# Graph layer 1 of a four-layer kernel: the row terms by sums on VectorE, a tile's own block of comparisons made by groups ahead, and part of the mask sums taken with the mask

## The chip, the cores and the metric

One core of one Trainium2 chip runs the whole program. The metric is the device time of one execution in microseconds (us), the median of the runs shown. The engines are named as the profile names them: PE (TensorE matmul), PEld (its weight load), DVE (VectorE), ACT (ScalarE), POOL (GpSimd), SP (SyncE, which here only issues transfers). Each engine works through its own queue in order.

## The reference, cut to what matters

Four graph layers run one after the other on `x` (2708 x 128) with a matrix `adj` (2708 x 2708); every layer begins with `h = relu(layernorm(x))` and adds its output to `x`. Layer 0 has a sum over each node's four nearest neighbours beside `adj @ h`. The change is in layer 1:

```
XW = h @ W
s_col = XW @ a[0, :128];  s_row = XW @ a[0, 128:]
den = exp(leaky_relu(s_row[:, None] + s_col[None, :], 0.01))
num = adj @ den
att = where(num != 0, den / num, 0)
x = x + adj @ (att @ XW)
```

`s_row` and `s_col` hold one number for each node. In the kernel they are called the row term (`r_nat`, node on the partition; `row_all`, the same numbers along the free axis, repeated on all partitions) and the column term (`c_nat`).

## The kernel before, in words

The 2708 nodes are 22 tiles of 128 (the last has 20), and six groups of four tiles (the last has two, 148 nodes). `adj` comes transposed, so a row tile of 128 x 2708 numbers, 1354 KB, is one "chunk".

**Second aggregation of layer 0** (`aggregate(y2, done_l0, kept=4)`, L597). For 17 chunks PE multiplies as they arrive, then for five chunks that stay in SBUF it goes bank by bank (L255). After bank b it calls `done_l0(b-1)`: copy to SBUF on ACT (L564), turn back by four PE transposes (L222), add to `xs` on DVE (L558), layer norm (L171 to L181), late neighbour terms (L524, gathered by POOL, L518), and `terms` of the group before.

**Row terms** (`terms`, L570). A group of `h1` is transposed on PE and copied to `hT` (L211, L214); a product with `rep`, the vector W a[128:] repeated 128 times (L429), gives the row term on every partition (L577), which ACT copies to `row_all` (L578); four PE transposes of one row bring it back to nodes on partitions (L580), in one PSUM bank that DVE copies to `r_nat` when all six groups are there (L599, L600).

**Places** (`place`, L656, for t = 0 to 21). The kernel sorts the nodes by row term by counting. DVE makes a 0/1 mask of the comparisons of tile t with itself and with all later tiles: the own block in two instructions with ties by node number (L662, L665), the rest in one (L669). ACT sums the mask along the row (L670, `later`). PE sums it down the columns into PSUM, bank by bank (L677). After each group of four tiles `places_of` copies one row of the counts (L690), turns it (L694), adds (L701, L706) and POOL scatters the nodes to their places in DRAM (L711, 22 scatters). The sorted list comes back at L822 and is turned at L824.

**Totals** (`total`, L736). Between the places PE forms `w_n @ adj` chunk by chunk (L744), with `w_n` from ACT (L635), which needs `r_nat` and its maximum. Nine chunks are still in SBUF (four in the pool `big`, five in row buffers); 13 are loaded again (L733): one at once into a free layer buffer, four into `big`, eight into the five row buffers, each load after the total that frees its buffer. Ten totals go with t = 1 to 10, one with each even t after that, the rest behind the places.

**Column terms** (`column_terms`, L754): 22 PE products of one column (L757), copied by DVE to `c_nat` (L758, L759). They are written after place 4, but the planner, which orders each engine's instructions by what is ready, puts them among the last row terms.

**Knots.** After the last total, DVE and ACT finish `tots` (L857, L858), four small transfers put it into `first` (its other parts are set by memsets, L859 to L861), and 22 gathers of sorted rows (L843) feed PE (L933) to the end of that loop; its first product needs the sorted list, `tots` and `first`.

`pin` keeps an instruction at its place in program order; the others are ordered by the planner.

Of the kernel before, what the change touches and what calls it, by code (L numbers as in the profile page):

```python
# [9 lines left out]
F32 = mybir.dt.float32  # L10
# [15 lines left out]
def kernel(  # L26
# [136 lines left out]
    def layernorm_relu(dst, g):  # L163

        t0, t1 = GROUPS[g]
        n = t1 - t0
        st = small.tile([P, 4, 6], F32, name="ln_st")
        mv = small.tile([P, 4, 2], F32, name="ln_mv")
        rs = small.tile([P, 4], F32, name="ln_rs")
        for t in range(t0, t1):  # L170
            nc.vector.bn_stats(st[:, t - t0, :], xs[:, t, :])  # L171
            nc.vector.bn_aggr(mv[:, t - t0, :], st[:, t - t0, :])
        root = nc.scalar.activation(rs[:, :n], mv[:, :n, 1], AF.Sqrt, bias=ln_eps)
        nc.vector.reciprocal(rs[:, :n], rs[:, :n])
        nm = small.tile([P, 4], F32, name="ln_nm")
        nc.vector.scalar_tensor_tensor(
            nm[:, :n], mv[:, :n, 0], -1.0, rs[:, :n], op0=ALU.mult, op1=ALU.mult
        )
        for t in range(t0, t1):
            o = t - t0  # L180
            nc.scalar.activation(  # L181
                dst[:, t, :],
                xs[:, t, :],
                AF.Relu,
                scale=rs[:, o : o + 1],
                bias=nm[:, o : o + 1],
            )
        return root
# [145 lines left out]
    for i in range(T):  # L334
# [4 lines left out]
        for b, (k0, n) in enumerate(KBS):  # L339
# [5 lines left out]
                start=(i == 0),  # L345
                stop=(i == T - 1),
            )
    sum_rows = res.tile([P, 1024], F32, name="sum_rows")
    for half, p0, p1 in ((0, 0, 128), (1, 0, 32 * (NKB - 5)), (1, 32 * (NKB - 5), 32 * (NKB - 4))):
        n = KBS[4 * half + p0 // 32][1]  # L350
        evacuate(sum_rows[p0:p1, 512 * half : 512 * half + n], sums[half][p0:p1, :n])
# [67 lines left out]

    wgT = consts.tile([P, P], F32, name="wgT")  # L420
    wga = consts.tile([P, 2], F32, name="wga")
    rep = consts.tile([P, P], F32, name="rep")
    p = ps_s.tile([P, 512], F32, name="ps")
    pin(nc.tensor.transpose(p[:, :P], wg, ident))
    nc.vector.tensor_copy(wgT, p[:, :P])
    p = ps_s.tile([P, 512], F32, name="ps")
    nc.tensor.matmul(p[:, :2], wgT, a_nat, start=True, stop=True)
    nc.vector.tensor_copy(wga, p[:, :2])
    nc.vector.tensor_scalar(rep, ones, wga[:, 1:2], None, op0=ALU.mult)  # L429

    top_v = keep.tile([P, T, 8], F32, name="top_v")
    top_i = keep.tile([P, T, 8], U32, name="top_i")
    strips = []
    nc.vector.memset(top_v[:, T - 1, :], 0.0)
    for t in range(T):
# [17 lines left out]
            nc.vector.max_index(top_i[:w, t, :], top_v[:w, t, :], s[:w, :])  # L455


    near_u = keep.tile([P, T, TOPK], U32, name="near_u")
    near_t = small.tile([P, T, TOPK], U32, name="near_t")

    def row_numbers(w, t0, t1):
# [7 lines left out]
        pin(nc.vector.max_index(top_i[:w, t, :], top_v[:w, t, :], strips[t][:w, :]))  # L469


    sim = keep.tile([P, T, TOPK], F32, name="sim")
    pin(
        nc.vector.scalar_tensor_tensor(
            sim, top_v[:, :, :TOPK], -2.0, sq.to_broadcast([P, T, TOPK]), op0=ALU.mult, op1=ALU.add
# [30 lines left out]
    row_numbers(TAIL, T - 1, T)  # L506


    simd = keep.tile([P, T, TOPK], F32, name="simd")
    nc.vector.tensor_tensor(  # L510
        simd, sim, dinv2[:, :, None].to_broadcast([P, T, TOPK]), ALU.mult
    )
# [1 line left out]
    def add_near(t, late=False):  # L514
        w = width(t)
        for k in range(TOPK):
            g = res.tile([P, D], F32, name="gath", bufs=32)
            nc.gpsimd.indirect_dma_start(  # L518
                out=g[:w, :],
                out_offset=None,  # L520
                in_=ydr[:, :],
                in_offset=bass.IndirectOffsetOnAxis(ap=near_u[:w, t, k : k + 1], axis=0),
            )
            term = nc.vector.scalar_tensor_tensor(  # L524
                xs[:w, t, :],
                g[:w, :],
                simd[:w, t, k : k + 1],
                xs[:w, t, :],
                op0=ALU.mult,
                op1=ALU.add,  # L530
            )
            if late and k == 0:
                pin(term)
# [25 lines left out]
            xs[:w, t, :], p, dinv2[:w, t : t + 1], xs[:w, t, :], op0=ALU.mult, op1=ALU.add  # L559
        )  # L560

    def to_h1(g, s2):
        k0, n = KBS[g]
        nc.scalar.copy(u2T[:, k0 : k0 + n], s2[g][:, :n])  # L564
        node_product(u2T, None, g, add_l0)
        return layernorm_relu(h1, g)

    r_ps = []

    def terms(g):  # L570
        t0, t1 = GROUPS[g]
        k0, n = KBS[g]
        if not r_ps:
            r_ps.append(acc(0))
        transposed(hT, h1, g, nc.scalar.copy)
        p = ps_s.tile([P, 512], F32, name="ps")
        nc.tensor.matmul(p[:, :n], rep, hT[:, k0 : k0 + n], start=True, stop=True)  # L577
        last = nc.scalar.copy(row_all[:, k0 : k0 + n], p[:, :n])  # L578
        for t in range(t0, t1):
            nc.tensor.transpose(  # L580
                r_ps[0][: width(t), t : t + 1], row_all[:1, cols(t)], ident[:1, :1]
            )
        return last


    late = {0: (15,), 1: (16,), 2: (17,), 3: (18, 19), 4: (20, 21)}

    def done_l0(g, s2):
        to_h1(g, s2)
        for t in late.get(g, ()):  # L590
            add_near(t, late=True)
        if g:
            terms(g - 1)

    for t in range(15):
        add_near(t)
    aggregate(y2, done_l0, kept=4)  # L597
    last_row = terms(NG - 1)
    pin(nc.vector.tensor_copy(r_nat[:, : T - 1], r_ps[0][:, : T - 1]))  # L599
    nc.vector.tensor_copy(r_nat[:TAIL, T - 1 :], r_ps[0][:TAIL, T - 1 : T])  # L600

    with tc.issue_after(last_row.ins):
        tables = nc.scalar.preload_act_table_set("natural_log_exp_and_others")
# [23 lines left out]
        nc.vector.tensor_reduce(top, p, AX.X, ALU.max)  # L627
        return top

    rmax = node_max("rmax", r_nat, r_ps[0][:, 256:384])  # L630
    r_n = vec("r_n")
    nc.vector.tensor_scalar(r_n, r_nat, rmax, None, op0=ALU.subtract)
    w_n = vec("w_n")
# [22 lines left out]
    def place(t):  # L656
        w = width(t)
        rt = r_nat[:w, t : t + 1]
        a, e = t * P, t * P + w
        mk = flags.tile([P, N], BF16, name="mask")  # L660
        eq = small.tile([P, P], F32, name="eq")
        nc.vector.scalar_tensor_tensor(  # L662
            eq[:w, :w], row_all[:w, a:e], rt, tri[:w, :w], op0=ALU.is_equal, op1=ALU.mult
        )
        nc.vector.scalar_tensor_tensor(  # L665
            mk[:w, a:e], row_all[:w, a:e], rt, eq[:w, :w], op0=ALU.is_le, op1=ALU.subtract
        )
        if e < N:
            nc.vector.tensor_scalar(mk[:w, e:], row_all[:w, e:], rt, None, op0=ALU.is_le)  # L669
            nc.scalar.activation(  # L670
                seen[:w, e:], mk[:w, e:], AF.Copy, accum_out=later[:w, t : t + 1]
            )
        for b, (k0, n) in enumerate(KBS):
            c0, c1 = max(a, k0), k0 + n
            if c0 < c1:
                g = 32 * (b % 4)
                nc.tensor.matmul(  # L677
                    cnt[b // 4][g : g + 32, c0 - k0 : c1 - k0],
                    ones_b[:w, :32],
                    mk[:w, c0:c1],  # L680
                    start=(t == 0),
                    stop=(e == c1),
                )

    def places_of(b):
        t0, t1 = GROUPS[b]
# [36 lines left out]
    def total_chunk(t, n):  # L723
        if t in resident:
            return resident.pop(t)
        if n == 0:
            c = lay.tile([P, N], F32, name="chunkY", tag="Y")
        elif n <= 4:
            c = big.tile([P, N + 1], F32, name="chunk", tag="big")
        else:  # L730
            c = rowtile("chunk")
        w = width(t)
        pin(nc.sync.dma_start(c[:w, :N], adjT[t * P : t * P + w, :]))  # L733
        return c
# [14 lines left out]
                    stop=(x_ == T - 1),  # L749
                )  # L750

    early = {todo[len(here)]: total_chunk(todo[len(here)], 0)}

    def column_terms():  # L754
        for t in range(T):
            w = width(t)
            nc.tensor.matmul(c_ps[:w, t : t + 1], hT[:, cols(t)], wga[:, 0:1], start=True, stop=True)  # L757
        nc.vector.tensor_copy(c_nat[:, : T - 1], c_ps[:, : T - 1])  # L758
        nc.vector.tensor_copy(c_nat[:TAIL, T - 1 :], c_ps[:TAIL, T - 1 : T])  # L759
        cmax = node_max("cmax", c_nat, c_ps[:, 384:512])  # L760
        nc.vector.tensor_scalar(cmx, cmax, rmax, -1.0, op0=ALU.add, op1=ALU.mult)
        c_n = vec("c_n")
        nc.vector.tensor_scalar(c_n, c_nat, rmax, None, op0=ALU.add)
        nc.vector.tensor_scalar(hb, c_n, 0.0, -0.495, op0=ALU.max, op1=ALU.mult)
        nc.scalar.activation(s_n, c_n, AF.Exp, scale=0.99)
        nc.scalar.activation(sig, hb, AF.Exp)
# [4 lines left out]
    for t in range(T):  # L771
        place(t)
        if t % 4 == 3 or t == T - 1:
            places_of(t // 4)
        if t == 4:
            column_terms()
        if 1 <= t <= len(here) + 1 or t % 2 == 0 and t:
            total(done)
            done += 1
    for x_ in range(done, T):  # L780
        total(x_)
    assert not resident
# [44 lines left out]
    nc.vector.tensor_copy(src_u[:PER, :], p[:PER, :T])  # L827
    nc.vector.tensor_copy(rs, p[:, T : 2 * T])

    moving = []

    def row_place():
        m = big.tile([P, N + 1], F32, name="mov", tag="big")
        moving.append(m)
        return m

    def fetch(t):
        m = moving[t] if t < len(moving) else row_place()  # L840
        if t:
# [8 lines left out]
        )  # L850


    first = row_place()
    tots = spare.tile([P, QUARTER], F32, name="tots", tag="spare")
    for half in range(2):
        x0 = tots[:, SPLIT * half : (SPLIT, QUARTER)[half]]
        nc.scalar.copy(x0, tot[half][:, : x0.shape[1]])  # L857
        nc.vector.scalar_tensor_tensor(x0, x0, 0.0, x0, op0=ALU.is_equal, op1=ALU.add)  # L858
    nc.vector.memset(first[0:1, :N], 0.0)  # L859
    nc.vector.memset(first[:, N : N + 1], 0.0)  # L860
    nc.vector.memset(first[0:1, N : N + 1], 1.0)  # L861
    for g in range(4):
        (nc.scalar, nc.sync)[g % 2].dma_start(
            first[1:2, QUARTER * g : QUARTER * (g + 1)], tots[32 * g : 32 * g + 1, :]
# [326 lines left out]
```

## Time and profile before

| | us |
|---|---|
| median of 3 runs | 1315.3 |
| lowest, highest | 1312.87, 1323.94 |
| profiled execution | 1309.14 |
| its span, first to last instruction | 1307.1 |
| PE busy in the span | 1085.9 |
| DVE busy | 560.4 |
| ACT busy | 411.7 |
| POOL busy | 228.1 |

All places in time below are us from the start of that span. The second aggregation runs from 349 to 543, the row terms from 526 to 561, the places and totals from 561 to 620, the knots from 630 to 787. A line of the table of windows gives for a stretch the busy time and the count of instructions of each engine, the clock that PE was granted (1.00 is full speed), the share of the DMA engines and their rate. A line of the timeline gives the start, the length, the engine, the line, the operation, the tiles, how many were merged, and in brackets how long the engine had been idle before and what ended that.

### The profile page before, as it was taken

Reading aid. Unit: us, or ns where it says so; the run is one execution under the profiler, and the core shown is the slowest. Engines: PE = TensorE matmul, PEld = TensorE weight load, DVE = VectorE, ACT = ScalarE, POOL = GpSimd, SP = SyncE. Lnnn points to the kernel's source line nnn. Section 1 sums busy time; section 2 is a strip of 40 time slices with the busy share of each in tenths; the row PEclk is TensorE's granted clock in tenths of the full one; section 3 lists DMA queues with packets and bytes.
Section 4 is the critical chain, followed back from the end, with each engine's and each line's share of the span. In section 5 each row is a group of like instructions: output and inputs, shape, how many; then the busy total and the mean of one; then the engine's idle time right before and its main releaser. Section 6 shows DMA issues by size and latency. Waiting matters only on the chain.

```text
span 1307.1 us, 10178 instructions
## 1 busy us (share of the span) xinstructions
PE 1085.9 (83%) x3623; PEld 510.2 (39%) x3623; DVE 560.4 (43%) x1178; ACT 411.7 (31%) x647; POOL 228.1 (17%) x188
## 2 busy tenths in 40 slices
PE   4889999999683359997777780687789999999998
PEld 1334444444240124553433330233344445545444
DVE  2020026999822000674465664899960031113003
ACT  3100014444400000585666743678830021003000
POOL 0100000000077720024211103567400000000000
PEclk8989999999795559887898985889989999999999
DMA  8997700000472242157999988999939916742831
GB/s 321 425 384 271 282 0 1 1 1 1 180 301 95 95 159 107 43 231 283 266 381 373 385 344 340 425 426 419 342 150 420 351 64 240 266 175 85 302 123 42
DMA packets 39505, 297.30 MB, mean 227 GB/s; under 512 B 6749, under 2 KB 10680, under 8 KB 13116
## 3 DMA queue, kind: packets, MB, share of 16 engines
q1 hardware_dynamic: 23806, 201.04, 40.2%
q0 software_dynamic: 13216, 93.62, 18.9%
q10 hardware_dynamic: 2434, 2.01, 0.6%
q8 instruction: 28, 0.46, 0.1%
q14 instruction: 21, 0.17, 0.0%
HBM read 264.46 MB, written 32.87 MB: 227 GB/s over the span
## 4 chain that ended last, share of the span: by engine, by line
PE 58%; DMA 18%; DVE 11%; issue 6%; another core or an unknown queue 6%; ACT 0%; POOL 0%; SPq 0%; ACTq 0%; DVEq 0%; POOLq 0%
PE acc L255 37%; DMA mov<-in_adj_dram,src_u 8%; PE acc L442 8%; DVE hi L1028 4%; DVE hi L1016 4%; DMA chunk<-in_adj_dram 3%; DMA hi<-table,hi_u 2%; PE acc L448 2%; PE acc L933 2%; PE ps L744 2%; DMA res<-in_adj_dram 2%; PE ps L224 1%; PE acc L1038 1%; PE ps L222 1%
## 5 line engine op out<-in xcount | busy, mean ns | idle before, releaser
L255 PE MATMUL acc<-chunk,y 128*128 128x512 f32 (+1 forms) x408 | 180.5, 592 | 73.2 <-issue 60.4
L1038 PE MATMUL acc<-hi,xw 128*128 128x512 f32 (+2 forms) x264 | 115.6, 594 | 65.6 <-DVE hi L1028 65.6
L255 PE MATMUL acc<-chunk,h 128*128 128x512 f32 (+1 forms) x384 | 148.0, 542 | 0.0
L255 PEld LDWEIGHTS acc<-chunk,y 128*128 128x128 f32 x408 | 79.6, 205 | 174.1 <-issue 162.4
L933 PE MATMUL acc<-mov,wt 128*128 128x512 f32 (+1 forms) x264 | 117.5, 600 | 34.7 <-DMA mov<-in_adj_dram,src_u 34.7
L518 POOL DMA_INDIRECT gath<-ydr,near_u x88 | 83.5, 949 | 346.5 <-DMA ydr<-y 320.0
L442 PE MATMUL acc<-zT 128*128 128x512 f32 (+2 forms) x264 | 107.6, 552 | 0.0
L1038 PEld LDWEIGHTS acc<-hi,xw 128*128 128x128 f32 (+1 forms) x264 | 52.1, 205 | 129.0 <-DVE hi L1028 69.3
L937 DVE COPY mov<-acc 2x512 f32<-2x512 f32 (+1 forms) x126 | 74.4, 611 | 63.8 <-PE acc L933 62.1
L255 PEld LDWEIGHTS acc<-chunk,h 128*128 128x128 f32 x384 | 68.8, 190 | 74.1 <-issue 74.1
L933 PEld LDWEIGHTS acc<-mov,wt 128*128 128x128 f32 x264 | 52.0, 208 | 96.3 <-issue 81.8
L451 ACT COPY strip<-acc 128x512 f32<-128x512 f32 (+2 forms) x132 | 60.5, 557 | 71.1 <-issue 58.5
L255 PE MATMUL acc<-chunk,attended 128*128 128x512 f32 x192 | 73.4, 545 | 0.0
L970 POOL DMA_INDIRECT lo<-table,lo_u x22 | 56.9, 2587 | 75.0 <-DVE hi L1016 34.5
L442 PEld LDWEIGHTS acc<-zT 128*128 128x128 f32 (+1 forms) x264 | 46.7, 186 | 56.8 <-issue 35.7
L938 ACT COPY knots<-acc 128x512 f32<-128x512 f32 x88 | 50.1, 587 | 59.0 <-DVE mov L937 42.2
L1016 DVE SCALAR_TENSOR_TENSOR hi<-lo,lam,hi 128x2708 f32<-128x2708 f32 (+4 forms) x25 | 67.2, 2697 | 1.0
L1028 DVE SCALAR_TENSOR_TENSOR hi<-row_all,inv_s,hi 128x2708 f32<-128x2708 f32 (+4 forms) x25 | 67.0, 2693 | 0.0
L1020 ACT ACTIVATE hi<-hi,lam 128x2708 f32<-128x2708 f32 (+4 forms) x25 | 56.7, 2280 | 32.4 <-issue 23.3
L453 DVE MAX8 top_v<-strip 128x8 f32<-128x2708 f32 (+1 forms) x22 | 64.6, 2965 | 0.5 <-ACT strip L451 0.4
L455 DVE FIND_INDEX8 top_i<-top_v,strip 128x8 uint32<-128x2708 f32 x20 | 59.2, 2973 | 0.0
L255 PE MATMUL acc<-res,h 128*128 128x512 f32 (+1 forms) x144 | 58.9, 551 | 0.0
(252 smaller groups left out, 1153.0 us busy)
## 6 DMA issues: line engine op xcount, KB each, us to landing
chunk<-in_adj_dram SPq DMA_DIRECT2D x111, 1354.0 KB
table<-knots SPq DMA_DIRECT2D x20, 1354.5 KB
res<-in_adj_dram SPq DMA_DIRECT2D x9, 1354.0 KB
ydr<-y SPq DMA_DIRECT2D x2, 704.0 KB
gath<-ydr,near_u POOLq DMA_INDIRECT x88
chunkY<-in_adj_dram SPq DMA_DIRECT2D x1, 1354.0 KB
table<-knots SPq DMA_DIRECT2D x1, 1333.3 KB
out_dram<-xs SPq DMA_DIRECT2D x5, 256.0 KB
```

Of the source, the lines that this page charges most:

```text
L255: nc.tensor.matmul(out[b][:, :n], y[:w, i, :], chunk(i)[:w, k0 : k0 + n], start=(i == 0), stop=(i == T - 1),)
L442: mm = nc.tensor.matmul(zz[b][:w, :n], zT[:, cols(t)], zT[:, k0 : k0 + n], start=True, stop=False)
L451: nc.scalar.copy(s[:w, k0 : k0 + n], zz[b][:w, :n])
L453: nc.vector.max(top_v[:w, t, :], s[:w, :])
L455: nc.vector.max_index(top_i[:w, t, :], top_v[:w, t, :], s[:w, :])
L518: nc.gpsimd.indirect_dma_start(out=g[:w, :], out_offset=None, in_=ydr[:, :], in_offset=bass.IndirectOffsetOnAxis(ap=near_u[:w, t, k : k + ...
L933: nc.tensor.matmul(p[:, :n], wt[:, t, :], moving[t][:, k0 : k0 + n], start=True, stop=True)
L937: nc.vector.tensor_copy(moving[t + 1][:2, k0 : k0 + n], p[:2, :n])
L970: nc.gpsimd.indirect_dma_start(out=dst[:w, :], out_offset=None, in_=table[:, :], in_offset=bass.IndirectOffsetOnAxis(ap=idx[:w, t : t + 1] ...
L1016: nc.vector.scalar_tensor_tensor(num, lo[:w, c], kap, num, op0=ALU.mult, op1=ALU.add)
L1028: nc.vector.scalar_tensor_tensor(att[:w, c], row_all[:w, c], inv_s[:w, t : t + 1], att[:w, c], op0=ALU.max, op1=ALU.mult,)
L1038: nc.tensor.matmul(py[b][:, :n], xw[:w, t, :], att[:w, k0 : k0 + n], start=(t == 0), stop=(t == T - 1),)
```

## The change

- The vector W a[128:] is laid along the free axis of every partition (`wrow`). A group's row terms are a product with it and a sum on DVE, from `h1` as it stands, straight into `r_nat`. `row_all` comes from PE transposes of `r_nat` repeated 128 times, with one copy on ACT. `hT` is still made, behind it.
- The own blocks (`own`, in bf16) are made by groups in four DVE instructions, for groups 0 to 3 while the aggregation ends, for groups 4 and 5 at t = 5 and t = 9 of the places. `place` only makes the mask of later tiles. The counts of the own block are PE products of their own.
- For every fourth tile (t = 2, 6, 10, 14, 18) DVE sums the mask with the instruction that makes it; ACT sums the others.
- The column terms are pinned at t = 12 of the places.
- Two chunks are loaded early (the second into the layer buffer `U`), four go to `big`, seven to the row buffers; one more total goes inside the places. `first` and its memsets are written before the last totals.
- The gather buffers of the neighbours go from 32 to 24, the late terms of tiles 20 and 21 behind the aggregation; a few tiles move between pools.

```diff
-    rep = consts.tile([P, P], F32, name="rep")
+    wrow = consts.tile([P, P], F32, name="wrow")
...
-    nc.vector.tensor_scalar(rep, ones, wga[:, 1:2], None, op0=ALU.mult)
+    nc.tensor.matmul(
+        p[:, P : 2 * P], wga[:, 1:2].to_broadcast([P, P]), ident, start=True, stop=True
+    )
+    nc.vector.tensor_copy(wrow, p[:, P : 2 * P])
...
-            g = res.tile([P, D], F32, name="gath", bufs=32)
+            g = res.tile([P, D], F32, name="gath", bufs=24)
...
     def terms(g):
-        transposed(hT, h1, g, nc.scalar.copy)
+        prod = res.tile([P, 4, D], F32, name="prod", tag="prod", bufs=2)
+        nc.vector.tensor_tensor(
+            prod[:, : t1 - t0, :],
+            h1[:, t0:t1, :],
+            wrow[:, None, :].to_broadcast([P, t1 - t0, D]),
+            ALU.mult,
+        )
+        e = min(t1, T - 1)
+        nc.vector.tensor_reduce(r_nat[:, t0:e], prod[:, : e - t0, :], AX.X, ALU.add)
...
-        nc.tensor.matmul(p[:, :n], rep, hT[:, k0 : k0 + n], start=True, stop=True)
-        last = nc.scalar.copy(row_all[:, k0 : k0 + n], p[:, :n])
         for t in range(t0, t1):
+            w = width(t)
+            o = (t - t0) * P
             nc.tensor.transpose(
-                r_ps[0][: width(t), t : t + 1], row_all[:1, cols(t)], ident[:1, :1]
-            )
+                p[:, o : o + w], r_nat[:w, t : t + 1].to_broadcast([w, P]), ident[:w, :w]
+            )
+        return nc.scalar.copy(row_all[:, k0 : k0 + n], p[:, :n])
+
+    def own_tiles(g, pool=res, tag="prod"):
...
+            same = nc.vector.tensor_tensor(eq, rows_, mine, ALU.is_equal)
...
+            nc.vector.tensor_tensor(
+                eq, eq, tri[:w, None, :w].to_broadcast([w, n, w]), ALU.mult
+            )
+            o = own[:w, c0:c1, :w]
+            nc.vector.tensor_tensor(o, rows_, mine, ALU.is_le)
+            nc.vector.tensor_tensor(o, o, eq, ALU.subtract)
...
+    for t in range(GROUPS[-1][0], T):
+        add_near(t, late=True)
+    layernorm_relu(h1, NG - 1)
     last_row = terms(NG - 1)
-    pin(nc.vector.tensor_copy(r_nat[:, : T - 1], r_ps[0][:, : T - 1]))
-    nc.vector.tensor_copy(r_nat[:TAIL, T - 1 :], r_ps[0][:TAIL, T - 1 : T])
+    transposed(hT, h1, NG - 1, nc.scalar.copy)
...
-        nc.vector.scalar_tensor_tensor(
-            eq[:w, :w], row_all[:w, a:e], rt, tri[:w, :w], op0=ALU.is_equal, op1=ALU.mult
-        )
-        nc.vector.scalar_tensor_tensor(
-            mk[:w, a:e], row_all[:w, a:e], rt, eq[:w, :w], op0=ALU.is_le, op1=ALU.subtract
-        )
+        count(own[:w, t, :w], a, e, True)
         if e < N:
+            mk = flags.tile([P, N], BF16, name="mask")
+            if t % 4 == 2:
+                nc.vector.tensor_scalar(
+                    mk[:w, e:],
+                    row_all[:w, e:],
+                    rt,
+                    0.0,
+                    op0=ALU.is_le,
+                    op1=ALU.add,
+                    accum_out=later[:w, t : t + 1],
+                )
...
-        if n == 0:
-            c = lay.tile([P, N], F32, name="chunkY", tag="Y")
-        elif n <= 4:
+        if n < 2:
+            c = lay.tile([P, N], F32, name="chunk" + "YU"[n], tag="YU"[n])
+        elif n < 6:
...
-        if t == 4:
+        if t in (5, 9):
+            own_tiles(NG - 2 + t // 9, spare, "spare")
+        if t == 12:
             column_terms()
-        if 1 <= t <= len(here) + 1 or t % 2 == 0 and t:
+        if 1 <= t <= len(here) + 2 or t % 2 == 0 and t:
             total(done)
...
+    first = row_place()
+    pin(nc.vector.memset(first[0:1, :N], 0.0))
```

## The prediction

> **What bounds the kernel now.** I read the chain of the page first: PE holds 58% of it, DMA 18%, DVE 11%. Then I cut the span into stages with the table of windows, and read the chain in order of time and the timeline of each engine between 510 and 630 us, where the change lies. The planner's order of the changed program, engine by engine, gave the queues; every duration is from a row of before.
>
> Stages (columns: busy us and count of PE, PEld, DVE, ACT, POOL, then clock, DMA share, GB/s):
>
> ```profile
> core 0: us, PE busy (x) PEld busy (x) DVE busy (x) ACT busy (x) POOL busy (x), PEclk, DMA share, GB/s
> ...
> 387.00:480.00 93.00, 32.74 (x38) 10.43 (x37) 13.99 (x41) 0.00 (x0) 60.63 (x65) 0.52 0.27 87
> ...
> 520.00:545.00 25.00, 25.00 (x102) 12.68 (x100) 15.36 (x72) 13.09 (x31) 0.00 (x0) 1.00 0.04 9
> 545.00:562.00 17.00, 14.52 (x66) 11.12 (x66) 9.35 (x42) 7.44 (x16) 0.00 (x0) 0.59 0.17 70
> 562.00:590.00 28.00, 25.37 (x277) 13.78 (x275) 23.81 (x53) 23.79 (x30) 9.71 (x8) 0.88 0.73 297
> 590.00:622.00 32.00, 22.77 (x208) 11.68 (x208) 14.65 (x55) 17.29 (x28) 14.81 (x16) 0.79 0.71 264
> ```
>
> To see: while the row terms are made (520 to 562) PE is the full engine and DVE works 24.7 of 42 us. In the first half of the places PE and DVE are both nearly full, in the second half neither.
>
> The chain from the places to the knots:
>
> ```profile
> 606.01 2.31 DVE mov L859
> 609.71 2.92 PE ps L744 x16
> 612.65 6.30 DMA chunk<-in_adj_dram
> 622.21 2.12 DMA mov<-tots
> ```
>
> To see: the places' last part runs into a memset on DVE, and the last chunk is loaded only at 612.65, because its buffer is freed late. Beside it, four us or less from being the later one, runs POOL:
>
> ```profile
> 575.18 1.61 POOL L711 DMA_INDIRECT order_d<-pay,to_u  x1 [108.04 <-DVE to_u L706]
> ...
> 605.57 0.98 POOL L711 DMA_INDIRECT order_d<-pay,to_u  x1 [2.40 <-DVE later L701]
> ...
> 611.96 0.90 POOL L711 DMA_INDIRECT order_d<-pay,to_u  x1 [0.30 <-issue]
> 616.04 0.58 POOL L822 DMA_DIRECT2D srtT<-order_d  x1 [3.18 <-DMA order_d<-pay,to_u]
> ```
>
> To see: six scatters follow the fourth group's result at 605.1 at 1.28 us each, then the list is read back; PE turns it at 620.27, just behind the last total. Both paths end together, so a gain needs both.
>
> **The change part by part.**
>
> *Row terms and own blocks, 521 to 566.* The prices:
>
> ```profile
> L191 DVE TENSOR_TENSOR y<-y,dinv x6: 418/684/694, 93.3 to 96.3; 128x512 f32<-128x512 f32 x5, 128x256 f32<-128x256 f32 x1
> L808 DVE TENSOR_TENSOR ge<-q,starts x1: 1099/1099/1099, 778.9 to 778.9; 128x924 f32<-128x924 f32 x1
> L815 DVE TENSOR_REDUCE qt<-ge x1: 1093/1093/1093, 780.5 to 780.5; 128x44 f32<-128x924 f32 x1
> ```
>
> L191 has the shapes of the six products; in the timeline the six take 3.44 us together, 0.61 each for 512. A sum costs what a product does (1.09 against 1.10 us for 924 numbers), so the six sums are 3.4 us. The own blocks of groups 0 to 3 are 16 instructions of 0.61 = 9.8, and one of group 4 stands ahead of the places, 0.6. Added on DVE: 17.2 us; gone are four copies (L758, L759, L599, L600), 0.5. DVE's idle time there is 42 - 24.7 = 17.3. From the first L558 at 521.2 the work is 24.7 + 17.2 - 0.5 = 41.4 us, to 562.6 without a gap. Gaps remain where DVE stands at a product that waits for ACT's `h1` of the same group (0.4 to 0.7 each in the first groups, and the last group's chain DVE, ACT, DVE, PE, ACT, some 2 us): I take 3 us, so the last `r_nat` is at 565.6 and, a transpose and a copy later, the first mask at 566.4 against 561.36 (L669): **+5.0**. Bounds: +1.5 without any gap, +8 with twice the gaps.
>
> PE loses L577 (8.4 us), L580 (2.6) and here L757 (6.6), and gains 22 transposes of L211's form, 0.60 for four, 3 us. That is worth nothing: DVE is later than PE from the third group on. The copies to `hT` move behind `row_all` on ACT, 0.6 each, hidden in the same way. Where the old stall goes: the first PE products wait for masks, and `w_n`, on ACT behind the table load and the first mask sum, comes 3.9 us after the first mask (565.30 against 561.36), so the first total moves from 565.7 to about 571, and with it the release of the first chunk buffer on SP's queue (568.57). Two chunks are on their way before that instead of one, and 3.4 us of transfer for one chunk at about 400 GB/s makes up for most of it.
>
> *The places.* DVE loses the two own-block instructions of each tile, which come at a pitch of 0.26 and 0.27 us: 22 x 0.53 = 11.6. It gains the rest of groups 4 and 5: three at 0.61 and some 1.2 of small ones, 3.0. The five masks with a sum have no row. Lower end: as L669 without it, 0. Upper end: one number a cycle, as L1028 has it against L952 (3.03 against 1.62 us for 2708 numbers): 1.41 x 6500/2708 = 3.4. I take 3.4, because the one DVE instruction shown that sums (L815) goes at that rate. Net on DVE: -11.6 + 3.0 + 3.4 = **-5.2**.
>
> The Trainium skill, page "VectorE: DVE Perf Modes", section "The perf-mode tier table", gives a fp32 `tensor_scalar` in SBUF two numbers a cycle and `tensor_reduce` one, and says nothing of one with a sum; its "Rules for kernel authors" advise against `tensor_reduce` on a hot path, which speaks against this change. By the page's rate for `tensor_scalar` the 3.4 would be 0 and the sum below lower by about 2; the rows of sums decide here.
>
> ACT loses five sums, 2.14 + 1.71 + 1.29 + 0.86 + 0.43 and five reads of 0.19 = 7.4 us; nothing, since ACT waited 3.5 and 4.1 us for masks there. PE gets the column terms inside the places: 12 take 2.74 us (24 records at 544.03), so 22 take 5.0; and 21 counts more, 0.1 to 0.23 each, 2 to 5 us. Behind them on DVE's queue: the copies of `c_nat` (two instructions that wait for PE) stand ahead of the masks of t = 16 to 21, so a late PE holds those masks, their counts and POOL's last six scatters.
>
> Step by step: masks t = 0 to 12 took 561.4 to 586.5. Now 13 x 0.53 = 6.9 less, 3.0 and 2.8 (t = 2, 6, 10) more: 24.0, to 590.4. PE then has a total (1.5) and the column terms: ready at about 597.0; DVE, done with t = 15 at 593.5, waits 3.5. From t = 15 to the fourth group's result before took 593.9 to 605.1 = 11.2. Now 6 x 0.53 = 3.2 less; the column terms' small DVE work with a PE step between, 1.7 more: 597.2 + 11.2 - 3.2 + 1.7 = 606.9, **+1.8**. POOL's six scatters end at 614.9 against 612.9, and the list is turned 2 us later.
>
> *Totals, loads, memset.* The total of t = 20 frees the buffer of the last load but one at about 608, the next one at 610 that of the last; with the 6.30 us of the chain it lands at 616.3, and the last total ends at 617.7 against 619.8. The memset (2.31) stands behind the last scatter's numbers on DVE. Both gains are covered by the scatters' path.
>
> *Elsewhere.* `wrow` is one PE product of 128 columns (0.3) and a copy of 0.29 in place of one of 0.29, where DVE is full with the strips: 0. With 24 gather buffers the last four gathers (1.25 us each on POOL) wait until 525, when tile 15 is added, and are needed at 559; POOL has nothing behind them until the places. 0, but see the rivals.
>
> **Sum.** +2 us on the path of the scatters. Low end: start +1.5, and DVE's whole 5.2 returned: -4. High end: start +8, column terms 5.0 and counts 3 in full, less 3.2: +13. Against the profiled execution (1309.14: span 1307.1 and 2.0 around it): 1311. That execution lies 6.2 under the median of 1315.3, so I forecast a median of **1317**. One per cent, 13 us, is about what a measurement of this kernel can tell from no change.
>
> **The rivals.**
>
> *The column terms hold DVE in full* (+5 to +13, 1320 to 1328, say 1324). For it: PE is busy 25.4 of 28 us in 562 to 590. Against: 22.8 of 32 after it, where they fall.
>
> *The row terms are not late* (-2 to -10, say 1307): the change does what its words say, DVE's 5.2 and the memset's 2.3 come through. Limit: 22 scatters of 1.28 from the first at 575.2 end no earlier than 603, 10 us less. Against: DVE's 17.3 idle us against 17.2 added.
>
> *Slower by over 1%: PE's slow stretch.* From 389 to 471 PE starts one recorded matmul each 2.80 us:
>
> ```profile
> 398.52 1.01 PE L255 MATMUL acc<-chunk,y 128*128 128x512 f32 x1 [1.80 <-issue]
> ...
> 401.31 1.01 PE L255 MATMUL acc<-chunk,y 128*128 128x512 f32 x1 [1.78 <-issue]
> ```
>
> Normal is 0.43. Each us more of it loses 0.85, so from 16 us more it costs over 13; say 1335. For it: nothing in the profile says what starts it, and the places too have PE, DVE, ACT and DMA busy at once. Against: the runs shown lie within 1% of each other.
>
> *It gets shorter.* It fades 3 to 12 us after the last gather (466.23). If gathers keep it up, four fewer (5 us) give -4, inside the range; were it gone, 82 x 0.85 = -70, 1247.
>
> The skill's page "TensorE: Matmul & The Clock Gate", section "Seeing it yourself", tells of a gate seen stuck at K=1/4 for over 50 us; the granted clock in the row is 0.52. By the page the stretch would be a state of the clock, no matter of gathers, and the -4 would be 0.
>
> **How the numbers follow.** Forecast as worked (-1 to +5): 0.50. Column terms in full: 0.22. Row terms not late: 0.15. Stretch longer: 0.07. Stretch much shorter: 0.06; the last two lie outside 1%, and a tenth or so of the column rival does: faster 0.06, slower 0.10, same 0.84. The range of 1306 to 1330 leaves out both stretch cases and the outermost ends, less than 0.2; within it the signs are mixed, and the likeliest case alone is 1314 to 1320.
>
> **What would show it.** DVE busy over 38 of the 42 us from 521; first mask 565 to 568; first total 570 to 572; the five masks with sums at one number a cycle (2.6 us for t = 2); a DVE wait for PE's column terms near 593 to 597; no memset between the last masks; last scatter near 614; last total before the list. Wrong if the first mask stays at 561, if DVE waits over 8 us at `c_nat`, or if the stretch of 387 to 480 changes its length.

## The result and the profile after

| | before | after |
|---|---|---|
| median, us (20 runs each) | 1318.63 | 1326.16 |
| lowest, highest | 1309.56, 1324.97 | 1320.06, 1333.93 |
| profiled execution, span | 1309.14, 1307.1 | 1321.62, 1319.8 |

The ratio is 1.0052, interval 1.0031 to 1.0073: about 7 us slower. The forecast was 1317 in a range of 1306 to 1330. Runs of one kernel spread over 15 us, and the profiled executions lie 9.5 us (before) and 4.5 us (after) under their medians. So below I read durations, waits and order from single profiles, and take times from the ratios.

The table of windows of after, for the stretches shown of before (columns as there):

```profile
core 0: us, PE busy (x) PEld busy (x) DVE busy (x) ACT busy (x) POOL busy (x), PEclk, DMA share, GB/s
387.00:480.00 93.00, 36.30 (x51) 12.52 (x50) 15.47 (x45) 0.00 (x0) 61.75 (x66) 0.56 0.28 92
520.00:545.00 25.00, 22.48 (x81) 10.91 (x79) 19.05 (x75) 10.22 (x24) 3.62 (x4) 0.98 0.08 24
545.00:562.00 17.00, 7.62 (x30) 5.62 (x30) 16.88 (x50) 7.12 (x16) 0.00 (x0) 0.50 0.34 132
562.00:590.00 28.00, 21.75 (x238) 12.26 (x238) 24.54 (x47) 19.61 (x24) 7.64 (x5) 0.77 0.53 214
590.00:622.00 32.00, 28.35 (x182) 18.54 (x180) 8.68 (x32) 7.58 (x20) 9.27 (x10) 0.68 0.50 206
```

Where the row terms are made, the full engine has changed: DVE is busy 16.88 of 17 us from 545 and PE 7.62 (9.35 and 14.52 before). In the last window it is the other way round: PE 28.35 of 32 us at a clock of 0.68, DVE 8.68. DVE's work in the places was cut, but DVE stands waiting for most of that window.

DVE's timeline of after, the row terms and the first masks:

```profile
528.73 0.70 DVE L579 TENSOR_TENSOR prod<-h,wrow 128x512 f32<-128x512 f32 x1 [0.37 <-ACT h L181]
...
531.38 0.65 DVE L586 TENSOR_REDUCE r_nat<-prod 128x4 f32<-128x512 f32 x1
...
567.63 1.56 DVE L728 TENSOR_SCALAR mask<-row_all,r_nat 128x2580 bf16<-128x2580 f32 x1 [0.78 <-ACT row_all L598]
569.31 1.49 DVE L728 TENSOR_SCALAR mask<-row_all,r_nat 128x2452 bf16<-128x2452 f32 x1
570.86 2.63 DVE L718 TENSOR_SCALAR_CACHE_REDUCE mask<-row_all,r_nat 128x2324 bf16<-128x2324 f32 x1
```

The product and the sum of a group cost nearly the same, 0.70 and 0.65; the mask with a sum takes 2.63 us for 2324 numbers, against 1.49 for 2452 without. Now the column terms, on PE, on DVE and on POOL:

```profile
600.93 9.24 PE L810 MATMUL acc<-wga,h1T 128*128 128x1 f32 x43
```

```profile
601.13 0.62 DVE L728 TENSOR_SCALAR mask<-row_all,r_nat 128x660 bf16<-128x660 f32 x1 [2.75 <-PE acc L706]
610.24 0.18 DVE L814 COPY c_nat<-acc 128x21 f32<-128x21 f32 x1 [8.50 <-PE acc L810]
```

```profile
619.01 0.97 POOL L763 DMA_INDIRECT order_d<-pay,to_u  x1 [15.56 <-DVE later L753]
...
631.86 0.90 POOL L763 DMA_INDIRECT order_d<-pay,to_u  x1 [0.30 <-issue]
637.16 0.58 POOL L893 DMA_DIRECT2D srtT<-order_d  x1 [4.41 <-DMA order_d<-pay,to_u]
```

44 passes (43 of them recorded in the first row) take 9.24 us on PE, DVE stands 8.50 at `c_nat`, and POOL waits 15.56 for the numbers of the next scatter. The last scatter is issued at 631.86 (611.96 before). The chain of waits runs through just these:

```profile
601.00 9.17 PE acc L810 x43
...
631.86 4.52 DMA order_d<-pay,to_u
637.16 1.90 DMA srtT<-order_d
641.04 2.13 DMA mov<-tots
```

In this pair of profiles the knots' `mov<-tots` comes 18.8 us later (641.04 against 622.21) but the span is only 12.7 longer: 4.8 us came back in the gathers of the knots, the rest near the end.

### The profile page after: what moved, and what is told of

It is laid out like the page before. It is cut to its first block, busy times and chain, and to the rows that moved or that the text cites. A ratio compares the mean times of both kernels' runs of the same rounds, so it can differ in the third digit from the quotient of the medians.

```text
span 1319.8 us, 10191 instructions
## 1 busy us (share of the span) xinstructions
PE 1095.2 (83%) x3629; PEld 516.7 (39%) x3629; DVE 571.7 (43%) x1178; ACT 404.8 (31%) x637; POOL 228.5 (17%) x188
## 4 chain that ended last, share of the span: by engine, by line
PE 56%; DMA 17%; DVE 12%; issue 8%; another core or an unknown queue 5%; POOL 1%; ACT 0%; SPq 0%; POOLq 0%; DVEq 0%; ACTq 0%
PE acc L255 36%; DMA mov<-in_adj_dram,src_u 8%; PE acc L445 8%; DVE hi L1086 3%; DVE hi L1074 3%; DMA chunk<-in_adj_dram 3%; PE acc L451 2%; PE acc L991 2%; DMA hi<-table,hi_u 2%; DMA res<-in_adj_dram 2%; PE ps L224 1%; PE ps L341 1%; PE acc L1096 1%; DMA xs<-in_x_dram 1%
## 5 line engine op out<-in xcount | busy, mean ns | idle before, releaser
L1096 PE MATMUL acc<-hi,xw 128*128 128x512 f32 (+2 forms) x264 | 119.0, 610 | 60.9 <-DVE hi L1086 60.9
```

Source lines behind the costliest of these rows:

```text
L1096: nc.tensor.matmul(py[b][:, :n], xw[:w, t, :], att[:w, k0 : k0 + n], start=(t == 0), stop=(t == T - 1),)
```

## The experiments

Ratios are to the kernel before, on the same chip; e1 to e4, e5 to e8 and e9 to e12 ran on three different chips, so ratios of two groups are compared across chips. 1% is 13.2 us.

**e1, e2, e5: the column terms moved, in the changed kernel.** Theory: they are what costs. Rivals: the row terms' tail on DVE, or the masks with sums.

```diff
-        if t == 12:
+        if t == T - 1:        # e1, still pinned
```

> The changed kernel with the 22 column products, still pinned, moved from t = 12 to behind the last place (t = 21). Theory (the column terms stand in VectorE's queue ahead of the masks of t = 17 to 21 and of the last scatters): no wait of 8.5 us at c_nat among the masks, fourth group's result near 607 and last scatter near 614 to 616 (631.9 now), knots begin near 627 to 630; time 1313 to 1319, so 0.996 to 1.000 of the kernel before. Rival A (the row terms' tail: VectorE full from 524 to 566 and a first mask 3 to 6 us later): the time stays at 1322 to 1327, ratio 1.003 to 1.006. Rival B (masks with sums at one number a cycle hold VectorE): the same 1322 to 1327.

Measured 1.0033, 1.0004 to 1.0062. The wait left the masks, as theory has it, but against the changed kernel (1.0052) the gain is 0.2%, about a quarter of what it forecast and within the noise. PE and the last load show why:

```profile
611.51 9.24 PE L810 MATMUL acc<-wga,h1T 128*128 128x1 f32 x43
...
633.16 1.35 PE L796 MATMUL ps<-chunk,w_n 128*32 128x338 f32 x16 [2.92 <-DMA chunk<-in_adj_dram]
```

The products now stand ahead of the remaining totals on PE; a total frees the buffer of the last load, so the last chunk lands late, and the last total starts at 633.16 with the list long there (its transfer was issued at 619.66).

```diff
-        if t == 12:
+        if t == 4:
...
-            pin(
-                nc.tensor.matmul(
+            nc.tensor.matmul(      # e2, not pinned
```

> The changed kernel with the column products at t = 4 and not pinned, as they stood in the kernel before. Theory: SBUF-to-PE work falls where the tensor engine is warm (granted clock 0.77 to 0.88 in 562 to 590), so the 44 passes take about 5 us instead of 9.2; the masks of t = 6 to 8 wait 2 to 5 us, but the scatters have slack there; last scatter 614 to 620, time 1315 to 1321 (0.997 to 1.002). Rivals A and B (row terms' tail, or masks with sums): 1322 to 1327.

Measured 0.9991, 0.9965 to 1.0018: 0.6% taken back, as the theory had it, though not by its path. Unpinned, all but the last few products went into PE's idle time among the row terms; the copy of `c_nat` at 571.07 waits for nothing, and no place waits for them.

```diff
+    def column_copies():       # called after the loop over the places
-        nc.vector.tensor_copy(c_nat[:, : T - 1], c_ps[:, : T - 1])
+        pin(nc.vector.tensor_copy(c_nat[:, : T - 1], c_ps[:, : T - 1]))
```

> The changed kernel with the column products where they are (pinned, t = 12), but the two copies to c_nat and what follows from them pinned behind the last place on VectorE. Theory 1 (the tensor engine is the shared queue: 9.2 us of column products hold back counts and totals, and with them the loads): the wait of 8.5 us at c_nat goes, but masks then wait for counts; last total and list move by 0 to 3 us; time 1322 to 1327, 1.003 to 1.006 of the kernel before. Theory 2 (VectorE's queue, blocked at c_nat, is what costs): the time falls to 1317 to 1320, 0.998 to 1.001.

Measured 1.0051, 1.0022 to 1.008. DVE no longer stands at `c_nat`, and the time is that of the changed kernel: theory 1. PE and DVE of this kernel:

```profile
595.41 4.96 PE L810 MATMUL acc<-wga,h1T 128*128 128x1 f32 x43
```

```profile
602.69 0.06 DVE L852 MEMSET mov<- 128x1 f32 x1 [5.38 <-PE acc L706]
```

The wait has changed its name: DVE waits 5.38 us for counts (L706) that stand behind the products on PE. The products took only 4.96 us here, against 9.24 in the changed kernel, at the same total time: the harm is not in proportion to their length. A common mark for all these kernels is when PE turns the sorted list, behind both paths: 113.8 us (e1), 114.3 (e5) and 115.2 (after) behind the first addition to `xs`, and 105.5 in e2, where the products are not pinned.

**e3, e12: the same pin in other kernels.** e3 puts it into the kernel before; e12 into e7 (below).

> The kernel before with one edit: the column products pinned at t = 12. Theory: PE takes 5 to 9 us for them, VectorE stands at c_nat for 4 to 9 us with nine masks behind it, so the last scatter goes from 612 to 617 to 622; time 1322 to 1328 (1.003 to 1.007). Rivals A and B: the edit is worth no more than 2 us, 1317 to 1321 (0.999 to 1.002).

Measured 0.9999, 0.9978 to 1.0021: no cost, the rivals' number. In the kernel before the products leave a stretch where PE is full, and the first mask comes 38.1 us after the first addition to `xs` (566.34 and 528.20) against 40.2. That gives back a part; the rest I can't show. In e3's one profile the forecast delay is there: PE takes 5.33 us for the products, DVE waits 4.56 at `c_nat`, and the list is turned 107.5 us behind the first addition, against 99.1 in before. That execution (1326.16) lies 5.2 us over its median, and the ratio shows nothing of the delay.

> The kernel of e7_own_in_place (0.9914) with the column products pinned at t = 12 again. Theory (44 passes on the tensor engine among counts and totals cost what they take there, 5 to 9 us, wherever the row terms do not gain from their leaving): 1315 to 1320, 0.995 to 0.999. Rival (as in the kernel before with the same edit, no cost): 1308 to 1312, 0.990 to 0.993.

Measured 0.9970, 0.9943 to 0.9997, against 0.9914 without the pin: +0.56%, theory. PE took 7.15 us and DVE waited 6.44.

**e4: loads and memset alone, in the kernel before** (two early chunks, four into `big`, one more total inside, `first` early; the diff is that part of the change).

> The kernel before with the loads, the extra total and the memset of the change alone (two chunks loaded at once, four into the big pool after them, totals with t = 1 to 11, memset written ahead of the remaining totals). My prediction put both gains behind the scatters' path, 0: 1317 to 1320 (0.999 to 1.001). If the last total and the scatters really end together and the memset of 2.3 us delays the last scatters, it gains 2 to 5 us: 1313 to 1317 (0.996 to 0.999).

Measured 0.9973, 0.9955 to 0.9991. Not covered, against my prediction.

**e6: the mask sums back on ACT**, on top of e2 (`t % 4 == 2` never taken).

> The changed kernel with column products at t = 4, not pinned (0.9991 before), and in addition all mask sums on ScalarE again. If the masks with sums cost what they add to VectorE in the places (3.4 us) it gains up to 3 us, 1313 to 1316 (0.996 to 0.999); if they are hidden, or ScalarE becomes late, no change, 1316 to 1320 (0.998 to 1.002).

Measured 0.9995, 0.9973 to 1.0016, against 0.9991 for e2. The masks with sums are neither a gain nor a loss.

**e7, e8: own blocks back in the places**, on top of e6; e8 also takes the loads and the memset back.

```diff
-        if g > 1:
-            own_tiles(g - 2)
...
-        count(own[:w, t, :w], a, e, True)
+        nc.vector.scalar_tensor_tensor(
+            eq[:w, :w], row_all[:w, a:e], rt, tri[:w, :w], op0=ALU.is_equal, op1=ALU.mult
+        )
+        nc.vector.scalar_tensor_tensor(
+            mk[:w, a:e], row_all[:w, a:e], rt, eq[:w, :w], op0=ALU.is_le, op1=ALU.subtract
+        )
...
-        if t in (5, 9):
-            own_tiles(NG - 2 + t // 9, spare, "spare")
```

> Row terms by sums on VectorE, early loads and memset, column products at t = 4 not pinned; but own blocks made tile by tile in the places as in the kernel before, mask sums on ScalarE. Theory (VectorE is full from 524 to 566, and own blocks of 10.4 us there are what delays the first mask): first mask 34 to 38 us after the first addition to xs (43.7 in the changed kernel, 40.2 before); time 1308 to 1315, 0.992 to 0.997. Rival (the loads of the last chunks set the end, whenever the masks begin): 1314 to 1319, 0.997 to 1.000.

Measured 0.9914, 0.9886 to 0.9942: better than hoped. But the first mask comes 41.4 us after the first addition (561.00 and 519.64), not 34 to 38: the theory's time came, its reason only in part (43.7 in the changed kernel).

> The kernel of e7_own_in_place without the early second load, the extra total and the early memset: what is left is row terms by sums, hT behind row_all, 24 gather buffers. If the row terms by sums bring the first mask 3 to 6 us forward and nothing else holds: 1311 to 1317 (0.994 to 0.998). Rival (last loads set the end): 1317 to 1321 (0.999 to 1.002).

Measured 0.9958, 0.9937 to 0.998. Beside e7 it prices loads and memset again, at 0.44%. Taken alone it looks like a gain of the row terms by sums; e9 says otherwise.

**e9, e10: the gather buffers.**

```diff
-            g = res.tile([P, D], F32, name="gath", bufs=32)
+            g = res.tile([P, D], F32, name="gath", bufs=24)   # e9, in the kernel before; e10: 16, in e7
```

> The kernel before with 24 gather buffers in place of 32, nothing else. From the first gather to the first addition to xs the three profiles of kernels with 32 buffers took 164.0, 165.7 and 166.3 us, the seven with 24 took 160.4 to 162.4. Theory (each gather inside the slow stretch keeps it up about 1 us; 24 buffers leave four gathers for later): about 161.5 us here, time 3 to 5 us less, 0.996 to 0.998 of the kernel before. Rival (the shift comes from another part of the change, or is scatter of the runs): 164 to 166 us and 0.999 to 1.001.

Measured 0.9954, 0.9926 to 0.9982; first gather to first addition 161.0 us (357.00 and 517.98), against 164.0 in before.

> The kernel of e7_own_in_place (0.9914) with 16 gather buffers in place of 24: eight gathers more leave the slow stretch. Theory: first gather to first addition about 153 to 155 us (161.6 there), time 6 to 8 us less than there, 1300 to 1305, 0.985 to 0.988. Rival (gathers do not set the length of the stretch, or the twelve late ones hold up the tail): 1308 to 1316, 0.990 to 0.996.

Measured 0.9859, 0.9823 to 0.9895; 151.4 us (357.45 and 508.84), 10.2 less than in e7, where 6.6 to 8.6 were forecast:

```profile
508.84 1.12 DVE L561 SCALAR_TENSOR_TENSOR xs<-ps,dinv,xs 128x128 f32<-128x128 f32 x4 [74.33 <-PE ps L222]
```

The first mask comes 10.8 us earlier (550.22 and 561.00), so what the stretch gave arrives there in full. In both kernels the time is the theory's (in e9 a little more than it). The windows around the last early gather, of before, of e9 and of e10:

```profile
460.00:470.00 10.00, 3.45 (x4) 1.15 (x4) 0.00 (x0) 0.00 (x0) 5.51 (x6) 0.50 0.08 24
470.00:480.00 10.00, 5.74 (x6) 1.73 (x6) 0.00 (x0) 0.00 (x0) 0.00 (x0) 0.50 0.35 123
```

```profile
460.00:470.00 10.00, 3.44 (x4) 0.86 (x3) 0.00 (x0) 0.00 (x0) 1.82 (x2) 0.50 0.44 158
470.00:480.00 10.00, 7.74 (x13) 3.39 (x13) 0.00 (x0) 0.00 (x0) 0.00 (x0) 0.67 0.41 152
```

```profile
460.00:470.00 10.00, 9.11 (x12) 3.54 (x12) 0.00 (x0) 0.00 (x0) 0.00 (x0) 0.52 0.81 313
470.00:480.00 10.00, 10.00 (x27) 4.68 (x26) 0.00 (x0) 0.00 (x0) 0.00 (x0) 1.00 0.98 392
```

The last gather before the aggregation's end starts at 466.23, 461.18 and 451.89. PE's count goes from 4 and 6 matmuls to 12 and 27 as POOL's column empties.

**e11: own blocks by groups, but inside the places**, on top of e6 (group 0 ahead of the first mask, group g+1 at t = 4g+1).

> The kernel of e6_t4_sums_act (own blocks by groups ahead, 0.9995) with the groups of own blocks moved out of the tail: group 0 ahead of the first mask, group g+1 at t = 4g+1. Theory A (own blocks in the full tail of VectorE cost): the first mask comes 2 to 4 us earlier, time 1310 to 1315, 0.992 to 0.996. Rival (their form costs: four instructions for a group, 22 counts of their own on the tensor engine): 1316 to 1321, 0.998 to 1.001.

Measured 0.9974, 0.9947 to 1.0001, between e7 and e6, and the first mask is not earlier: 44.6 us after the first addition (566.82 and 522.25), so theory A's reason fails. From the row maximum on (L663 here, L662 in e7), DVE of e11 and of e7:

```profile
563.51 0.18 DVE L663 TENSOR_REDUCE hi_n<-r_nat 128x1 f32<-128x22 f32 x1
563.61 0.68 DVE L609 TENSOR_TENSOR eq<-row_all,r_nat 128x512 f32<-128x512 f32 x1
...
565.40 0.68 DVE L612 TENSOR_TENSOR eq<-eq,tri 128x512 f32<-128x512 f32 x1
...
566.82 2.97 DVE L726 TENSOR_SCALAR mask<-row_all,r_nat 128x2580 bf16<-128x2580 f32 x2
```

```profile
559.12 0.18 DVE L662 TENSOR_REDUCE hi_n<-r_nat 128x1 f32<-128x22 f32 x1
559.21 0.60 DVE L704 SCALAR_TENSOR_TENSOR mask<-row_all,r_nat,eq 128x128 bf16<-128x128 f32 x2
560.80 0.29 DVE L665 TENSOR_REDUCE rmax<-acc 128x1 f32<-128x128 f32 x1 [0.98 <-PE acc L663]
561.00 1.55 DVE L708 TENSOR_SCALAR mask<-row_all,r_nat 128x2580 bf16<-128x2580 f32 x1
```

A group's own blocks go in one lump ahead of the first mask, 3.3 us against 1.9. Two fused instructions of one tile (pitch 0.27) are a little cheaper than a quarter of four plain ones (4 x 0.6 / 4 = 0.6 against 2 x 0.27 = 0.54): the grouping moves work ahead without making it less.

## Why the prediction was right in time, and where its steps were wrong

The runs make a ladder from the kernel before to the changed one, one part at a step. Each step is the difference of two ratios, uncertain by 0.3 to 0.35%:

| step | from, to | % | about us |
|---|---|---|---|
| 24 gather buffers | before, e9 | -0.46 | -6 |
| row terms by sums, `hT` behind | e9, e8 | +0.04 | 0 |
| loads, extra total, memset | e8, e7 | -0.44 | -6 |
| own blocks by groups | e7, e6 | +0.81 | +11 |
| mask sums on DVE | e6, e2 | -0.04 | 0 |
| column terms pinned at t = 12 | e2, after | +0.61 | +8 |
| all | before, after | +0.52 | +7 |

The +2 that I forecast became +7 out of four terms of 6 to 11 us of both signs, none of which my sum had at more than 2 us net. The time was in the range, but it was not the sum that put it there: that errors of both signs nearly cancelled is luck.

Two cautions on the ladder. Its steps hold in this order only: the parts do not simply add, since the pinned column terms cost 0.6% in two kernels (e2 to after, e7 to e12) and nothing in the kernel before (e3). And most steps are little larger than their uncertainty; each of the four large ones was found twice (gathers in e9 and e10; loads in e4 and e7; column terms in after and e12; own blocks in e6 and e2, both 0.8% above e7).

*Row terms and own blocks (+5.0 on the first mask).* The durations were right: 0.70 and 0.65 for products and sums, DVE 35.9 of 38.1 us busy from 523.9 to 562. From the first addition to the first mask it is 43.7 us against 40.2, +3.5, inside the bounds; the rest of the 6.3 between the two profiles stood ahead of it. The profiles of the runs divide the 3.5: it is 40.1 to 40.3 us in before, e4 and e9, 41.4 in e7, e8 and e10, which have the row terms by sums, and 43.7 in after, e1, e5 and e6 (44.4 in e2), which have the own blocks ahead as well. So the sums cost 1.3 us there and the own blocks 2.3. In time the row terms by sums are worth nothing (e8 against e9), and the own blocks cost 0.8%. "Net on DVE -5.2" in the places was taken as a return. It returned nothing that shows: e7, with all that work on DVE, is faster. The rows of after have DVE waiting there for PE, not full (8.68 of 32 us from 590).

*PE's removed products: 0.* Right as far as it was tested: e8 and e9, which differ by the products and the sums together, are equal. The Trainium skill's advice against `tensor_reduce` on a hot path ("VectorE: DVE Perf Modes", section "Rules for kernel authors") did not decide here: a sum of 512 numbers took 0.65 us, no longer than a product (0.70), and the exchange cost no time that shows.

*Masks with sums.* The size was right (2.63 us for t = 2), the effect nothing.

*Column terms (+1.8).* The step failed by size and by mechanism. I priced them at 5.0 us from a stretch where PE was warm and let DVE's queue carry the harm. They took 9.24 us at a granted clock of 0.50, DVE waited 8.5 (my text said: wrong if over 8), and e5 shows that DVE's wait at `c_nat` is not what costs. From the rows of e1 and e5 I take it that PE's order carries the harm: counts, totals and through these the loads stand behind 44 passes (the last total waits 2.92 and 4.43 us for its chunk). That is argued, not shown: e3 has the same passes at no cost, and no run has them at t = 12 without the pin. That was the rival "column terms hold DVE in full", with the wrong engine in its name; its +5 to +13 holds the measured +8.

*Totals, loads, memset: covered, 0.* Failed: 4 to 6 us came through (e4, e8 against e7). I read list and last total as ending together. But the profile of before already had the last total waiting for its chunk, and PE turning the list behind it without a wait, a row that my prediction left out:

```profile
618.99 1.35 PE L744 MATMUL ps<-chunk,w_n 128*32 128x338 f32 x16 [1.87 <-DMA chunk<-in_adj_dram]
620.27 0.29 PE L824 MATMUL acc<-ident,srtT 22*126 22x22 f32 x1
```

So the load was the later path there, and a gain on it could come through. In e9, the kernel before with other buffers, PE shows the same:

```profile
618.17 2.48 PE L744 MATMUL ps<-chunk,w_n 128*32 128x338 f32 x16 [3.90 <-DMA chunk<-in_adj_dram]
620.59 0.30 PE L824 MATMUL acc<-ident,srtT 22*126 22x22 f32 x1
```

The last total waits 3.90 us for its chunk, and the list is turned behind it without a wait: the load is the later path there. In e7, with the loads changed, the list is the later one:

```profile
614.53 3.02 PE L783 MATMUL ps<-chunk,w_n 128*32 128x339 f32 x34 [0.26 <-issue]
619.10 0.29 PE L876 MATMUL acc<-ident,srtT 22*126 22x22 f32 x1 [1.55 <-DMA srtT<-order_d]
```

*Gather buffers: 0.* Failed; the rival "it gets shorter" was right, with its reason and nearly its size (-4 forecast, -6 measured). In the changed kernel, too, first gather to first addition fell from 164.0 to 160.4 us. I had given it 0.06 because I priced it together with the whole stretch vanishing. The Trainium skill's account of a gate stuck at a low ratio ("TensorE: Matmul & The Clock Gate", section "Seeing it yourself") would have made e9 and e10 worth nothing; the measurements decide for the gathers.

*Open.* How the +0.8% of the own blocks arises and divides. It is more than the 2.3 us on the first mask. e11 puts about a quarter of it (0.2%) on their place ahead and the rest on the lump and the form, but the difference is within the intervals. In e6's profile DVE stands twice for a reason that no record shows ("remote": what ended the wait has no name in the profile):

```profile
590.34 0.69 DVE L742 COPY mine<-acc 1x512 f32<-1x512 f32 x1 [5.07 <-remote]
...
608.26 0.68 DVE L742 COPY mine<-acc 1x512 f32<-1x512 f32 x1 [6.72 <-remote]
```

PE, its only named releaser, is idle itself (7.18 us, waiting for this copy, until 608.99). e7 has none of these, after has 3.45 and 2.47, before 2.00. e6's 11.8 us are not what the own blocks cost: e2, the same kernel with five mask sums on DVE, has 1.1 us of them and is as slow (0.9991). But e8 has 8.5, so part of e8 against e7 may be theirs. An instruction transfer on queue q14 shows in the 2 us slices from 588 and from 602, but e7 has such transfers without a wait. Also open: why e3 cost nothing.

## What to carry to other kernels

When work is moved, price it by the queue it lands in, at the clock of that place, and follow everything behind it there; a wait that is taken off one engine (e5) comes back under another name as long as the shared queue holds. Cutting an engine's work pays only in a stretch where that engine ends last: look at what the last step of each path waits for, in more than one profile, before calling a gain covered. And build the parts singly: here two that gain (early loads, fewer gathers beside the matmuls) were hidden by two that lose, and the best kernel of the study is e10, with the row terms by sums, early loads, own blocks in place and 16 gather buffers: 0.9859, 1301.6 us.

## What the runs showed of the hardware

- From about 388 on, while POOL's gathers run (one per 1.25 us), PE starts most recorded 512-column matmuls 2.80 us apart instead of 0.43, with "issue" as the reason (it waits for nothing that the profile shows) and a granted clock of 0.50 to 0.56, too little to explain a factor of 6.5 (at 0.50 the 44 passes of the next point took 1.9 times as long as at 1.00). In e10, whose last early gather starts at 451.89, the timeline has the pitch at 2.80 to 457.84, then 2.10 and 1.41, and from 464.40 on 33 matmuls in 15.80 us. 88, 84 and 76 gathers ahead of the tail gave 1, 0.9954 and (e10 against e7) 0.9945 of the time. The gathers are not enough by themselves: in before they start at 357.13 at the same pace, and PE keeps its full rate and clock until 387, 86 matmuls in 32 us beside 24 gathers. The rows of before for that stretch and the slow one:

```profile
355.00:387.00 32.00, 32.00 (x86) 15.12 (x85) 7.16 (x21) 0.00 (x0) 22.86 (x24) 1.00 0.91 351
387.00:460.00 73.00, 23.56 (x29) 7.55 (x27) 13.99 (x41) 0.00 (x0) 55.11 (x59) 0.53 0.28 90
```

So the runs show that fewer gathers end the stretch sooner, by 10.2 us for eight (e10 against e7) and 3 to 5 for four (e9 against before, e3 and e4). What starts it and what couples the two engines is not shown.
- The 44 passes of one column took 4.96, 5.33, 7.15 and 9.24 us (e5, e3, e12, after). The granted clock in those stretches was 1.00, 0.93, 0.66 and 0.50: the product is 4.6 to 5.0 us each time. A duration on PE carries over only with its clock.
- A comparison with a sum on DVE takes about twice as long as one without (2324 numbers in 2.63 us; 2452 in 1.49 without), 1.04 ns for each further number (276 take 0.50), and reading the sum costs 0.08 more.
